# A four-layer graph network on one core: overflow records loaded in one piece, and the side work of a layer-1 block spread over the slots of the block before it

## The chip, the core and the metric

The kernel runs on one core of one Trainium2 chip. The metric is the device time of one execution in microseconds (us), the median of several executions. The core has five engines with an instruction queue each: TensorE (PE in the profile; PEld is its weight load), VectorE (DVE), ScalarE (ACT), GpSimd (POOL) and SyncE (SP), which here only issues transfers. An engine takes its queue in order: an instruction that waits holds up all that stands behind it.

## The reference, cut to what matters

A node table x of 3125 nodes with 256 numbers passes through four layers. Each layer adds a graph step, a mixing step and then a feed-forward step. The change touches the graph step of layer 1 and the preparation of its lists.

```
x   = x + L0_gnn(xn, src, dst) + L0_mix(xn);    x = x + L0_ffn(layernorm(x))
xn  = layernorm(x)
x   = x + L1_gnn(xn, edge_index, edge_type_7, weights) + L1_mix(xn)
x   = x + L1_ffn(layernorm(x))
...  # layers 2 and 3 likewise, with edge weights
```

The layer-1 graph step has 100000 edges of 7 types. Each node adds up, over its incoming edges, the source's row times the matrix of the edge's type, and divides what arrives by each type by the number of such edges (at least 1). Layers 2 and 3 need, for every node, the sums of two edge weights and a count over its incoming edges.

## The kernel before

The nodes are cut into NB = 25 blocks of BS = 125. Edges are held by block in slots of P = 128 edges. For layers 0, 2 and 3 a block has SL = 37 slots (25 regular, OV = 12 overflow); for layer 1 the edges are ordered anew, and a block has L1S = 34 slots (25 regular and 9 overflow).

**Overflow records.** Edges that do not fit layer 1's regular slots are written as records of four numbers to a table `lov_d` in device memory. They wait there in `lrec_d`, with their places in `lpos_d`. `scatter_overflow` (L2334, called 25 times from L2224 to L2225 in `fast_layer0`, ahead of `mix0`) loads 12 columns of places (`lpos`, L2337) and of records (`lrec`, L2339) through SP and then issues 12 indirect writes on POOL (L2341), 300 in all. The tiles have two buffers each. `mix0` follows in the same pool, and its PE, DVE and ACT work can run beside the writes. `lists1` reads `lov_d` back at the start of layer 1.

**Layer 1.** `fast_layer1` first multiplies all nodes by the seven matrices into a table `y_d` of N*7 rows. Then comes the loop of L2451 to L2466. For each of the 34 slots of a block it gathers 128 rows of `y_d` with an indirect transfer from POOL (`rows`, L2461, seen under the helper's line L665), makes a weighted one-hot matrix on DVE (`hot`, L2463), and multiplies the two on PE into the block's sum `agg` (L2465, two matmul records for a slot). After the 34 slots DVE adds `agg` to x (L2466). `rows` has 20 buffers and `hot` 8: the gather of a slot needs the matmul of 20 slots earlier to be done.

**Side work.** The weights of a block's slots, `l_w`, come from `weights1` (L2379 to L2421): seven groups of up to five slots, for each a one-hot `l_hot` on DVE (L2389, two buffers) and five matmuls (L2392) that count the types of each node; then one inversion of the counts (L2395 to L2404); then seven look-ups, each with a broadcast load `hotl` on SP (L1971), a comparison on DVE (L2411) and up to five matmuls (L2414); two multiplications and reductions to `l_w` (L2417, L2419). `node_sums` (L2238 to L2258) makes the sums that layers 2 and 3 need: eight groups with a one-hot `dsthot` on DVE (L2233) and up to five matmuls each (L2250, 37 in all), then a transpose and two small operations.

The loop is written so that the whole side work of block j stands before the slots of block j-1:

```
for j in range(NB + 1):
    if j < NB:
        ws[j] = weights1(k, gp, o, j)
        node_sums(k, gp, j)
    ...
    i = j - 1
    for s in range(L1S): ...   # gather, hot, matmul
```

A scheduler places the instructions of each engine, with the written order as priority and the readiness of their inputs as it models it; the pools decide which buffer an instruction must wait for. In the program as built, each engine's order differs from the written one. On PE, the counting matmuls L2392 of the coming block stand as one bunch of 34 at the end of a block's slots, and the look-ups and node sums stand in bunches of 5 to 20 among the slots of the next. DVE's order follows the same pattern. POOL's queue in the loop holds only gathers, and SP's only the `hotl` loads.

After the loop come the rest of `mix1` (a few of its first operations already lie within the last two blocks) and `ffn1`.

Of the kernel before, what the change touches and what calls it, by code (L numbers as in the profile page):

```python
# [7 lines left out]
F32 = mybir.dt.float32  # L8
BF16 = mybir.dt.bfloat16
I32 = mybir.dt.int32  # L10
AF = mybir.ActivationFunctionType
ALU = mybir.AluOpType
AX = mybir.AxisListType
# [4 lines left out]
D = 256  # L18
E = 100000
BS = 125  # L20
NB = N // BS
P = 128
# [458 lines left out]
def psum(k):  # L481
    return k.mm.tile([P, 512], F32, name="mm")
# [78 lines left out]
def bc(ap, shape):  # L561
    return ap.to_broadcast(shape)
# [1500 lines left out]
def fast_layer0(k):  # L2063
# [157 lines left out]
            if start is not None:  # L2221
                gathers(start)
    with tc.tile_pool(name="l0m", bufs=1) as mp:
        for i in range(NB):  # L2224
            scatter_overflow(k, mp, i)  # L2225
        mix0(k, mp, None, xt)
    ffn0(k)

# [9 lines left out]
def node_sums(k, pool, i):  # L2238

    nc, e = k.nc, k.e  # L2240
    ab = pool.tile([P, SL, 7], BF16, name="ns_ab", bufs=2)
    split3(k, pool, e.ew[:, i, :], ab[:, :, 0:3], [P, SL], "ns_a")
    split3(k, pool, e.ew1[:, i, :], ab[:, :, 3:6], [P, SL], "ns_b")
    nc.vector.memset(ab[:, :, 6:7], 1.0)
    ps = psum(k)
    for s0 in range(0, SL, LQ):
        n = min(LQ, SL - s0)
        hd = dst_hot(k, pool, i, s0, n)
        for u in range(n):
            nc.tensor.matmul(ps[:7, :BS], ab[:, s0 + u, :], hd[:, u, :BS], start=s0 + u == 0,  # L2250
                             stop=s0 + u == SL - 1)
    t = pool.tile([7, BS], F32, name="ns_t", bufs=2)
    nc.scalar.copy(t, ps[:7, :BS])
    pt = k.tp.tile([P, 4, P], F32, name="tp")
    nc.tensor.transpose(pt[:BS, 0, :7], t, k.ident[:7, :7])
    nc.vector.tensor_reduce(e.nd[:BS, i, 0:2], pt[:BS, 0, :6].rearrange("p (a t) -> p a t", t=3),
                            AX.X, ALU.add)
    nc.vector.tensor_copy(e.nd[:BS, i, 2:3], pt[:BS, 0, 6:7])  # L2258


def hot_src(k, pool, e, i, s0, n):
# [69 lines left out]
        nc.sync.dma_start(e.lrec_d, lrec)  # L2331


def scatter_overflow(k, pool, i):  # L2334
    nc, tc, e = k.nc, k.tc, k.e
    lpos = pool.tile([P, OV], I32, name="lpos", bufs=2)
    nc.sync.dma_start(lpos, e.lpos_d[:, i * OV:(i + 1) * OV])  # L2337
    lrec = pool.tile([P, OV, 4], F32, name="lrec", bufs=2)
    nc.sync.dma_start(lrec, e.lrec_d[:, i * OV:(i + 1) * OV, :])  # L2339
    for c in range(OV):  # L2340
        st = nc.gpsimd.indirect_dma_start(  # L2341
            out=e.lov_d, out_offset=bass.IndirectOffsetOnAxis(ap=lpos[:, c:c + 1], axis=0),
            in_=lrec[:, c, :], in_offset=None)
        tc.declare_no_dep(st.ins, group="scatter_l", reason="each edge has a place of its own")
        tc.add_to_no_dep_group("scatter_l", st.ins)
# [30 lines left out]
LG = 5  # L2376


def weights1(k, pool, o, j):  # L2379

    nc = k.nc
    oh = pool.tile([P, L1S, 7], BF16, name="ty_hot", bufs=2)
    nc.vector.tensor_tensor(oh, bc(o.ty[:, j, :, None], [P, L1S, 7]),
                            bc(k.iotab[:, None, :7], [P, L1S, 7]), op=ALU.is_equal)
    cnt = k.agg.tile([P, 512], F32, name="agg")[:7, :BS]
    for s0 in range(0, L1S, LG):
        n = min(LG, L1S - s0)
        S = pool.tile([P, LG, P], BF16, name="l_hot", bufs=2)
        nc.vector.tensor_tensor(S[:, :n, :], bc(o.slb[:, j, s0:s0 + n, None], [P, n, P]),  # L2389
                                bc(k.iotab[:, None, :], [P, n, P]), op=ALU.is_equal)  # L2390
        for u in range(n):
            nc.tensor.matmul(cnt, oh[:, s0 + u, :], S[:, u, :BS], start=s0 + u == 0,  # L2392
                             stop=s0 + u == L1S - 1)
    ct = pool.tile([7, BS], F32, name="l_ct", bufs=2)
    nc.scalar.copy(ct, cnt)  # L2395
    pt = k.tp.tile([P, 4, P], F32, name="tp")
    nc.tensor.transpose(pt[:BS, 0, :7], ct, k.ident[:7, :7])
    inv = pool.tile([BS, 7], F32, name="l_inv", bufs=2)
    nc.vector.tensor_scalar(inv, pt[:BS, 0, :7], 1.0, None, op0=ALU.max)
    nc.vector.reciprocal(inv, inv)  # L2400
    inv3 = pool.tile([BS, 7, 3], BF16, name="l_inv3", bufs=2)
    split3(k, pool, inv, inv3, [BS, 7], "l_i")
    w = pool.tile([P, L1S], F32, name="l_w", bufs=2)
    for h0 in range(0, L1S, 4 * LG):  # L2404
        m = min(4 * LG, L1S - h0)
        pw = psum(k)
        for s0 in range(h0, h0 + m, LG):
            n = min(LG, h0 + m - s0)
            ST = pool.tile([P, LG * P], BF16, name="hotl", bufs=3)
            bcast_rows(k, ST[:, :n * P], o.slT_d, j, s0, n)  # L2410
            nc.vector.tensor_scalar(ST[:, :n * P], ST[:, :n * P], k.part, None, op0=ALU.is_equal)  # L2411
            for u in range(n):
                c = s0 + u - h0
                nc.tensor.matmul(pw[:, c * 21:(c + 1) * 21], ST[:BS, u * P:(u + 1) * P],  # L2414
                                 inv3.rearrange("p a t -> p (a t)"), start=True, stop=True)
        t = pool.tile([P, 4 * LG, 7, 3], F32, name="l_t", bufs=2)
        nc.vector.tensor_tensor(t[:, :m], pw[:, :m * 21].rearrange("p (s a t) -> p s a t", a=7, t=3),  # L2417
                                bc(oh[:, h0:h0 + m, :, None], [P, m, 7, 3]), op=ALU.mult)
        nc.vector.tensor_reduce(w[:, h0:h0 + m], t[:, :m].rearrange("p s a t -> p s (a t)"), AX.X,  # L2419
                                ALU.add)  # L2420
    return w  # L2421


def fast_layer1(k):
    nc, tc, I = k.nc, k.tc, k.ins
    T = 7
    with tc.tile_pool(name="l1g", bufs=1) as gp:
        o = lists1(k, gp)
        xn, xt = k.fresh_norm(gp)
        y_d = k.dpool.tile([N * T, D], F32, name="y_d")  # L2430
        yv = y_d.rearrange("(n t) d -> n (t d)", t=T)
        with tc.tile_pool(name="l1y", bufs=1) as yp:
            wt = yp.tile([P, T, 2, D], F32, name="wt")
            nc.sync.dma_start(wt.rearrange("p t c o -> p (t c) o"),
                              I["L1_gnn_weights"].rearrange("(a p) o -> p a o", p=P))
            for b in range(NB):
                y = yp.tile([BS, T, D], F32, name="y", bufs=2)
                for t in range(0, T, 2):
                    n = min(2, T - t)
                    ps = psum(k)  # L2440
                    pv = ps[:BS, :n * D].rearrange("p (t d) -> p t d", d=D)
                    for c in range(2):
                        nc.tensor.matmul(pv, xt[:, c, b * BS:(b + 1) * BS], wt[:, t:t + n, c, :],
                                         start=c == 0, stop=c == 1)
                    evac(k, y[:, t:t + n, :], pv)
                rows_out(k, yv, b, y.rearrange("p t d -> p (t d)"))
        with tc.tile_pool(name="l1m", bufs=1) as mp:
            k.e.dlb = gp.tile([P, NB, SL], BF16, name="dlb")
            nc.vector.tensor_copy(k.e.dlb, k.e.dl)
            ws = {}  # L2450
            for j in range(NB + 1):  # L2451
                if j < NB:
                    ws[j] = weights1(k, gp, o, j)
                    node_sums(k, gp, j)
                if j == 0:
                    continue
                i = j - 1
                agg = k.agg.tile([P, 512], F32, name="agg")[:BS, :D]
                for s in range(L1S):
                    G = gp.tile([P, D], F32, name="rows", bufs=20)  # L2460
                    gather(k, G, y_d, o.yidx[:, i, s:s + 1])  # L2461
                    S = gp.tile([P, P], F32, name="hot", bufs=8)
                    nc.vector.tensor_scalar(S, k.iota, o.sl[:, i, s:s + 1], ws[i][:, s:s + 1],  # L2463
                                            op0=ALU.is_equal, op1=ALU.mult)
                    nc.tensor.matmul(agg, S[:, :BS], G, start=s == 0, stop=s == L1S - 1)  # L2465
                nc.vector.tensor_tensor(k.x[:, i, :], k.x[:, i, :], agg, op=ALU.add)  # L2466
            mix1(k, mp, xn, xt)
    ffn1(k)

# [84 lines left out]
def split3(k, pool, src, out, shape, name):  # L2554

    nc = k.nc
    r = pool.tile(shape, F32, name=name + "_r", bufs=2)
    nc.vector.tensor_copy(out[..., 0], src)
    nc.vector.tensor_tensor(r, src, out[..., 0], op=ALU.subtract)
    nc.vector.tensor_copy(out[..., 1], r)  # L2560
    nc.vector.tensor_tensor(out[..., 2], r, out[..., 1], op=ALU.subtract)  # L2561
# [260 lines left out]
```

## Time and profile before

| | us |
|---|---|
| Runs: median (lowest to highest of 3) | 9158.93 (9139.79 to 9187.19) |
| Profiled execution: its own time | 9142.26 |
| Span within it | 9140.2 |
| Overflow writes, first to last | 1995.1 to 2389 |
| Layer-1 loop, first gather to last matmul | 3110 to 4503 |

The profile gives for each engine its busy time and share of the span; a strip of 40 slices, each 228.5 us here, with the busy share in tenths; groups of instructions by line, with count, busy time, mean duration in ns and the idle time ahead of them with its releaser; a list of waits in a chosen stretch (engine, tile and line, what ended the wait, total, times, longest); a table of windows with the busy time of each engine, PE's granted clock, the DMA share and GB/s; and a timeline, with the start, the time, the engine and line, and in square brackets the idle time before an instruction and what ended it. "issue" is idle time in which the profile shows nothing waited for; "remote" is a release that it can't name. The layer-1 loop lies in slices 14 to 20 of 40.

### The profile page before, as it was taken

Reading aid. Unit: us, or ns where it says so; the run is one execution under the profiler, and the core shown is the slowest. Engines: PE = TensorE matmul, PEld = TensorE weight load, DVE = VectorE, ACT = ScalarE, POOL = GpSimd, SP = SyncE. Lnnn points to the kernel's source line nnn. Section 1 sums busy time; section 2 is a strip of 40 time slices with the busy share of each in tenths; the row PEclk is TensorE's granted clock in tenths of the full one; section 3 lists DMA queues with packets and bytes.
Section 4 is the critical chain, followed back from the end, with each engine's and each line's share of the span. In section 5 each row is a group of like instructions: output and inputs, shape, how many; then the busy total and the mean of one; then the engine's idle time right before and its main releaser. Section 6 shows DMA issues by size and latency. Waiting matters only on the chain. (4 is left out here: it accounts for less than half of the span.)

```text
span 9140.2 us, 90939 instructions
## 1 busy us (share of the span) xinstructions
PE 6246.5 (68%) x30915; PEld 4571.4 (50%) x30915; DVE 4900.0 (54%) x12476; ACT 1717.6 (19%) x4057; POOL 2252.8 (25%) x2188
## 2 busy tenths in 40 slices
PE   0736888871488755555577887649936666668899
PEld 0724666650244433333456666338825555555455
DVE  9966777751233344444654343741157777775311
ACT  0013444530111000000024444212200000002232
POOL 0001222237300266666402432020032222210000
PEclk9967999985677866766689998759967877779899
DMA  0013333320000333333202222035532222220000
GB/s 18 10 40 98 83 86 82 83 51 4 2 13 30 124 104 99 99 98 101 69 11 66 56 54 52 0 92 173 167 83 67 67 67 66 65 51 20 11 11 22
DMA packets 399982, 570.48 MB, mean 62 GB/s; under 512 B 129911, under 2 KB 322875, under 8 KB 395161
## 3 DMA queue, kind: packets, MB, share of 16 engines
q0 software_dynamic: 107456, 246.32, 12.0%
q1 hardware_dynamic: 292054, 318.25, 12.0%
q8 instruction: 249, 4.08, 0.2%
q14 instruction: 223, 1.83, 0.1%
HBM read 485.78 MB, written 78.47 MB: 62 GB/s over the span
## 5 line engine op out<-in xcount | busy, mean ns | idle before, releaser
L665 POOL DMA_INDIRECT rows<-y_d,l_yidx x850 | 861.1, 1013 | 1246.1 <-DMA kln_weight<-in_L_mix_kln_weight_dram 721.3
L2465 PE MATMUL agg<-rows,hot 128*125 128x256 f32 x1700 | 555.3, 470 | 107.0 <-DVE hot L2463 68.6
L665 POOL DMA_INDIRECT xt<-xp_d,e_idx x300 | 310.6, 1035 | 1135.6 <-PE agg L2704 999.4
L665 POOL DMA_INDIRECT rows<-h_d,e_idx x300 | 306.1, 1020 | 679.5 <-PE agg L2505 393.1
L2465 PEld LDWEIGHTS agg<-rows,hot 128*125 128x125 f32 x1700 | 354.6, 226 | 217.7 <-DVE hot L2463 86.6
L2139 PE MATMUL mm<-er,hotd 125*128 125x258 bf16 x1875 | 319.9, 278 | 193.5 <-DVE jk L2111 133.3
L2483 ACT ACTIVATE whot<-dsthot,e_ew 128x128 f32<-128x128 bf16 x925 | 333.1, 397 | 397.3 <-PE mm L2498 175.4
L2182 ACT ACTIVATE whot<-dsthot,prob 128x128 f32<-128x128 bf16 x925 | 358.8, 401 | 216.8 <-DVE jk L2111 75.7
L2233 DVE TENSOR_TENSOR dsthot<-dlb,iotab 128x640 bf16<-128x640 bf16 (+1 forms) x400 | 306.8, 771 | 130.1 <-remote 108.2
L2463 DVE TENSOR_SCALAR hot<-iota,l_sl,l_w 128x128 f32<-128x128 f32 x850 | 261.1, 363 | 196.8 <-PE agg L2465 130.3
L2502 PE MATMUL agg<-A,dense 125*125 125x256 f32 x1250 | 340.5, 428 | 30.0 <-DVE dense L76 15.4
L2183 PE MATMUL agg<-z,whot 128*125 128x257 f32 x1250 | 356.0, 426 | 6.1 <-ACT whot L2182 6.1
L2686 PE MATMUL mm<-A,hots 125*128 125x256 f32 x1250 | 352.0, 429 | 0.0
L2695 PE MATMUL agg<-msg,whot 128*125 128x260 f32 x1250 | 325.8, 399 | 30.8 <-DVE msg L2689 30.8
L2341 POOL DMA_INDIRECT lov_d<-lrec,lpos x300 | 302.8, 1009 | 152.0 <-issue 91.2
L665 POOL DMA_INDIRECT xn<-el_d,e_idx x156 | 165.1, 1058 | 678.0 <-PE agg L2183 345.9
L2139 PEld LDWEIGHTS <-hotd 125*128 125x128 bf16 x1875 | 181.4, 98 | 274.7 <-issue 224.1
L2617 PE MATMUL mm<-m,hotd 125*128 125x12 bf16 x925 | 28.8, 173 | 409.3 <-DVE m L2561 409.3
L1686 DVE SCALAR_TENSOR_TENSOR x<-mm,gate_lg,x 125x256 f32<-125x256 f32 x200 | 94.6, 484 | 398.8 <-PE mm L545 398.8
L2392 PE MATMUL agg<-l_hot,ty_hot 128*7 128x125 bf16 x850 | 102.9, 282 | 298.5 <-DVE l_hot L2389 223.8
L2111 DVE SCALAR_TENSOR_TENSOR jk<-mm,attn 128x258 bf16<-128x258 f32 x625 | 264.4, 423 | 79.1 <-ACT z L2144 37.6
L2502 PEld LDWEIGHTS agg<-A,dense 125*125 125x125 f32 x1250 | 258.6, 215 | 86.2 <-DVE dense L76 20.2
(683 smaller groups left out, 14262.4 us busy)
## 6 DMA issues: line engine op xcount, KB each, us to landing
w<-in_L_ffn_W_dram SPq DMA_DIRECT2D x64, 1024.0 KB
hotd<-dlT_d SPq DMA_DIRECT2D x25, 1184.0 KB
hotd<-dlT_d SPq DMA_DIRECT2D x175, 160.0 KB
hotl<-lslT_d SPq DMA_DIRECT2D x150, 160.0 KB
y_d<-y SPq DMA_DIRECT2D x25, 875.0 KB
hots<-slT_d SPq DMA_DIRECT2D x125, 160.0 KB
hots_r<-slT_d SPq DMA_DIRECT2D x150, 128.0 KB
rows<-y_d,l_yidx POOLq DMA_INDIRECT x850
```

The costliest lines, as they stand in the source:

```text
L665: k.nc.gpsimd.indirect_dma_start(out=out, out_offset=None, in_=table, in_offset=bass.IndirectOffsetOnAxis(ap=idx, axis=0))
L2111: nc.vector.scalar_tensor_tensor(jk, z, 0.0, at, op0=ALU.max, op1=ALU.mult, accum_out=b.score[:, s:s + 1])
L2139: nc.tensor.matmul(z, DT[:BS, u * P:(u + 1) * P], b.er3[:, j, :], start=j == 0, stop=False)
L2182: nc.scalar.activation(pd, hd[:, u, :], AF.Copy, scale=b.p[:, s:s + 1])
L2183: nc.tensor.matmul(b.agg, pd[:, :BS], rows[:, u, :D + 1], start=s == 0, stop=s == SL - 1)
L2233: k.nc.vector.tensor_tensor(t[:, :n, :], bc(k.e.dlb[:, i, s0:s0 + n, None], [P, n, P]), bc(k.iotab[:, None, :], [P, n, P]), op=ALU.is_equal)
L2341: st = nc.gpsimd.indirect_dma_start(out=e.lov_d, out_offset=bass.IndirectOffsetOnAxis(ap=lpos[:, c:c + 1], axis=0), in_=lrec[:, c, :], in_ ...
L2465: nc.tensor.matmul(agg, S[:, :BS], G, start=s == 0, stop=s == L1S - 1)
L2483: nc.scalar.activation(pd, hd[:, u, :], AF.Copy, scale=e.ew[:, i, s0 + u:s0 + u + 1])
L2502: nc.tensor.matmul(agg, A[:BS, u, :BS], hv[:, s0 + u, :], start=s0 + u == 0, stop=False)
L2686: nc.tensor.matmul(pg[:, (u - u0) * D:(u - u0 + 1) * D], STs[s0 // GQ][:BS, u * P:(u + 1) * P], av[:, s0 + u, :], start=True, stop=True)
L2695: nc.tensor.matmul(agg, pd[:, :BS], M[:, u, :], start=s0 + u == 0, stop=False)
```

## The change

1. `scatter_overflow` loads all 300 columns of `lpos` (128 x 300) and `lrec` (128 x 1200) with one transfer each, and then issues the same 300 indirect writes. The tiles have one buffer each.
2. `weights1` and `node_sums` no longer run their work but return it as steps: 7 count, 1 invert, 7 look, 1 begin, 8 add, 1 end, 25 in all. The loop places the steps of block j+1 between the slots of block j, 0 or 1 after each slot. Block 0's steps run ahead of the loop.
3. `rows` has 16 buffers instead of 20, `hot` 10 instead of 8, `l_hot` 3 instead of 2.

```diff
-        for i in range(NB):
-            scatter_overflow(k, mp, i)
+        scatter_overflow(k, mp)
...
-    lpos = pool.tile([P, OV], I32, name="lpos", bufs=2)
-    nc.sync.dma_start(lpos, e.lpos_d[:, i * OV:(i + 1) * OV])
-    lrec = pool.tile([P, OV, 4], F32, name="lrec", bufs=2)
-    nc.sync.dma_start(lrec, e.lrec_d[:, i * OV:(i + 1) * OV, :])
-    for c in range(OV):
+    C = NB * OV
+    lpos = pool.tile([P, C], I32, name="lpos")
+    nc.sync.dma_start(lpos, e.lpos_d)
+    lrec = pool.tile([P, C, 4], F32, name="lrec")
+    nc.sync.dma_start(lrec, e.lrec_d)
+    for c in range(C):
...
-        S = pool.tile([P, LG, P], BF16, name="l_hot", bufs=2)
+        S = pool.tile([P, LG, P], BF16, name="l_hot", bufs=3)
...
+    groups = list(range(0, L1S, LG))
+    return ([lambda s0=s0: count(s0) for s0 in groups] + [invert]
+            + [lambda s0=s0: look(s0) for s0 in groups])
...
+    return [begin] + [lambda s0=s0: add(s0) for s0 in range(0, SL, LQ)] + [end]
...
-            for j in range(NB + 1):
-                if j < NB:
-                    ws[j] = weights1(k, gp, o, j)
-                    node_sums(k, gp, j)
-                if j == 0:
-                    continue
-                i = j - 1
+            def side(j):
+                if j >= NB:
+                    return []
+                ws[j] = gp.tile([P, L1S], F32, name="l_w", bufs=2)
+                return weights1(k, gp, o, j, ws[j]) + node_sums(k, gp, j)
+            for f in side(0):
+                f()
+            for j in range(NB):
+                steps = side(j + 1)
                 agg = k.agg.tile([P, 512], F32, name="agg")[:BS, :D]
                 for s in range(L1S):
-                    G = gp.tile([P, D], F32, name="rows", bufs=20)
+                    G = gp.tile([P, D], F32, name="rows", bufs=16)
...
-                    S = gp.tile([P, P], F32, name="hot", bufs=8)
+                    S = gp.tile([P, P], F32, name="hot", bufs=10)
...
                     nc.tensor.matmul(agg, S[:, :BS], G, start=s == 0, stop=s == L1S - 1)
+                    n = len(steps) * (s + 1) // L1S - len(steps) * s // L1S
+                    for f in steps[len(steps) * s // L1S:len(steps) * s // L1S + n]:
+                        f()
```

In the program as built after the change, the largest bunch of side matmuls between two slots on PE holds 20 instead of 35, and most hold 5; the longest run of side operations between two `hot` on DVE is 6 instead of 24. POOL's order of writes and gathers is the one of before. SP has 48 transfers fewer. The block's addition to x stands on DVE ahead of the counting steps of the block after next.

## The prediction

> **What bounds the kernel now.** I read the page first: the totals, then the strip.
>
> ```profile
> span 9140.2 us, 90939 instructions
> PE 6246.5 (68%) x30915; PEld 4571.4 (50%) x30915; DVE 4900.0 (54%) x12476; ACT 1717.6 (19%) x4057; POOL 2252.8 (25%) x2188
> PE   0736888871488755555577887649936666668899
> POOL 0001222237300266666402432020032222210000
> ```
>
> No engine bounds the whole; each stage has its own limit. The change touches two stages: slices 8 to 10 (overflow writes) and 14 to 20 (layer-1 loop). In the loop POOL is at 6 tenths and PE at 5: neither is full. The groups give POOL's and PE's part of it.
>
> ```profile
> L665 POOL DMA_INDIRECT rows<-y_d,l_yidx x850 | 861.1, 1013 | 1246.1 <-DMA kln_weight<-in_L_mix_kln_weight_dram 721.3
> L2465 PE MATMUL agg<-rows,hot 128*125 128x256 f32 x1700 | 555.3, 470 | 107.0 <-DVE hot L2463 68.6
> ```
>
> 850 gathers of 1013 ns are 861 us of a loop of 1393 us (3110 to 4503). The 721.3 is the wait ahead of the first gather and is no part of the loop. The list of waits for that stretch says what POOL waits for (us in total, times, longest), and what PE waits for:
>
> ```profile
> POOL rows L665 <- PE agg L2465: 213.5, 128, 10.5
> POOL rows L665 <- issue: 168.4, 543, 1.9
> POOL rows L665 <- remote: 102.7, 95, 3.0
> ...
> PE agg L2392 <- DVE l_hot L2389: 221.7, 62, 17.6
> PE mm L2250 <- DVE dsthot L2233: 136.6, 27, 7.4
> PE agg L2392 <- issue: 72.7, 13, 12.0
> PE agg L2465 <- DVE hot L2463: 68.6, 51, 2.9
> ```
>
> "issue" is 0.3 us ahead of an ordinary gather. The longest waits are for the slot matmul L2465: no row buffer is free. And PE, which should free it, waits most in the side work. The timeline of POOL shows one such place, then the ordinary pace:
>
> ```profile
> 3304.85 0.98 POOL L665 DMA_INDIRECT rows<-y_d,l_yidx  x1 [9.48 <-PE agg L2465]
> 3306.13 0.95 POOL L665 DMA_INDIRECT rows<-y_d,l_yidx  x1 [0.30 <-issue]
> 3307.39 0.95 POOL L665 DMA_INDIRECT rows<-y_d,l_yidx  x1 [0.30 <-issue]
> ```
>
> PE and DVE ahead of it, from the same timeline:
>
> ```profile
> 3293.99 0.42 DVE L2466 TENSOR_TENSOR x<-x,agg 125x256 f32<-125x256 f32 x1 [7.82 <-remote]
> ...
> 3297.03 0.69 PE L2392 MATMUL agg<-l_hot,ty_hot 128*7 128x125 bf16 x5 [11.67 <-issue]
> ...
> 3303.36 1.22 PE L2465 MATMUL agg<-rows,hot 128*125 128x256 f32 x2 [1.32 <-DVE hot L2463]
> ```
>
> The slot matmul before that last line ended at 3284.2: 19 us with none. For 11.7 us PE stood in its bunch for an `l_hot` that was queued on DVE behind the addition to x, itself held 7.8 us by a release the profile can't name; 6.3 us more went to the rest of the bunch.
>
> So a gather can go every 1.25 us (0.95 + 0.30). By the starts of all 850, 21 of the 25 blocks have one wait of over 3 us, nearly always after the block's 20th gather: 20 buffers are full, and the block's first matmul is queued behind the 34 counting matmuls of the next block, which wait for `l_hot`. These 21 waits are 174 us beyond the 0.30 each. Another 45 waits of 1 to 3 us, mostly after the 31st gather, are 83 us. Longer gathers (1013 against 950 ns) are 54 us, the rest small. Typical block: 56.5 us, of which 42.5 (34 x 1.25) is POOL's floor.
>
> The windows say whether another engine would be next:
>
> ```profile
> 3600.00:4000.00 400.00, 211.62 (x1230) 148.59 (x1229) 191.59 (x555) 3.57 (x14) 241.96 (x239) 0.70 0.35 99
> ```
>
> Columns: length, busy PE, PEld, DVE, ACT, POOL, PE clock, DMA share, GB/s. Over the whole loop PE is busy 769 us (31 a block), DVE 671 (27 a block): both under 42.5.
>
> [...] the last gather starts at 4495.3 and its matmul is over at 4503.2, with seven slots of matmuls caught up in the last 5 us. I take up to 8 us from gather to matmul. [...] gathers last 0.95 us at the median, some 1.4 to 1.7. The DVE operations stay the same in number, so I keep those 54 us. [...] The trace has 0.70 in the loop, and a slot's matmul pair takes 0.70 or 1.22 us.
>
> **Part by part.**
>
> *Steps between slots.* Nothing is removed: 34 + 34 + 37 side matmuls and 7 + 7 + 8 wide one-hots a block stay, and so do the seven `hotl` loads on SP, whose queue in the loop holds nothing else. What changes is order. PE's longest bunch between two slot matmuls shrinks from 35 to 20, most to 5; DVE's longest side run between two `hot` from 24 operations to 6. Five matmuls behind one `l_hot` are 0.82 + 5 x 0.28 = 2.2 us; twenty are 20 x 0.18 to 0.28 = 4 to 6 us, and six DVE operations 3 to 4 us. With 16 buffers POOL runs 16 x 1.25 = 20 us ahead of PE; 8 of them cover the landing, 12 remain. Each of these bunches fits in 12, so the 6.3 us of bunch come off those 19, and the 11.7 us at the addition to x, which I leave as it is, plus 2.2 for the first five matmuls exceed the cover by about 2 us a block. The 174 us go, but some of that comes back: of the 83 us in the 45 shorter waits I take away only half, 41, and the 42 left are those 2 us a block. (DVE's waits at the addition to x are 24, 120 us, "remote", up to 12.2 each; all that follows on DVE is queued behind it, the next block's `hot` and `l_hot` above all, then PE, then POOL.) Sum: 174 + 41 = **215 us** off the loop, 1393 to 1178. A second way gives nearly the same. Block 25, beside which no next block's side work lies, took 46.6 us; 25 x 46.6 + 8 for the last landing = 1173. The floor is 25 x 42.5 + 54 + 8 = 1125, a gain of 268.
>
> *Buffers.* 16 `rows` for 20 take 4 x 1.25 = 5 us of cover. If a stall of more than 12 us is left in every block, each is 5 us longer than with 20: up to 25 x 5 = 125 us back. `hot` 10 lets DVE run 12.5 us ahead of POOL's pace instead of 10; `l_hot` 3 gives one group more. I take 0 for all three, with 0 to +125.
>
> *Block 0's steps* stay ahead of its slots, as before: 0. *mix1 and ffn1* start when the loop ends; their length doesn't change: 0.
>
> *Records in one piece.* 48 of SP's 50 transfers of 6 or 24 KB go. POOL never waits for them after the first: 300 writes go steadily at 1.28 us (0.97 + 0.30) from 1995.1 to 2389, and the only wait is before the first. That first write now waits for 154 + 614 KB; at the 99 GB/s of the window shown this is about 8 us, where the small pair took 3.7 (issued from 1991.4): 4 us later. And `mix0`'s weights are queued behind it on SP. The writes then end near 2393. `mix0` beside them goes on to about 2550, so 0 with that cover, +4 without it. On the other side: during the writes `mix0` crawls, with waits of up to 51 us on DVE and ACT whose releaser the profile can't name ("remote"), and its passes take 9.6 us each once the writes are over, against some 55. If the 25 small load pairs caused that, `mix0` would end with the writes: 2550 - 2393 = 157 us less. Nothing ties the two: loads come every 15.3 us, the waits last about 46. I take 0, with -157 to +4.
>
> Sum: -215 on the profiled execution's 9142.3 gives 8927. The median of the runs lies 17 us above that execution; I take half, and predict **8935**.
>
> **Rivals.**
>
> *(a) The coupling of DVE and PE becomes the pace: slower.* From 4457 to 4470 PE and DVE have little side work, and still a slot takes 2.1 to 3.6 us: DVE makes one `hot`, waits for PE, PE makes one slot and waits.
>
> ```profile
> 4459.91 0.35 DVE L2463 TENSOR_SCALAR hot<-iota,l_sl,l_w 128x128 f32<-128x128 f32 x1 [1.78 <-PE agg L2465]
> 4462.03 0.53 DVE L2463 TENSOR_SCALAR hot<-iota,l_sl,l_w 128x128 f32<-128x128 f32 x1 [1.77 <-PE agg L2465]
> 4464.87 0.35 DVE L2463 TENSOR_SCALAR hot<-iota,l_sl,l_w 128x128 f32<-128x128 f32 x1 [2.31 <-PE agg L2465]
> ```
>
> With side work after most slots, such a round trip could come at every step. Today a slot costs 1393 / 850 = 1.64 us in the mean; the rival decides from there. If half the slots took 2.4 and half 1.37 (46.6 / 34), the loop is 850 x 1.89 = 1607: +214, so 9142 + 214 = 9356. Against it: 10 `hot` buffers, and in most of the trace PE takes slots in runs of several.
>
> *(b) No change: landing sets the pace.* If rows land no faster than 1.6 us a slot, emptier queues gain nothing: 9142 to 9159. For it: waits called "remote" that may be late transfers. Against: the waits of `agg` for `rows` are 10.5 us in the whole loop, and the DMA share is 0.35. Nor would it be a change of the text that a scheduler undoes: the built order differs as said.
>
> *(c) mix0 is freed as well:* 8927 - 157 = 8770.
>
> **How the numbers follow.** A difference within 0.5%, about 46 us, is what a measurement of this kernel can tell from no change. Main case 0.77: gains of 80 to 268, so 8875 to 9080. (c) 0.08. (b) 0.07. (a) 0.08. Faster 0.77 + 0.08 = 0.85, same 0.07, slower 0.08. The range reaches down to 8820, for a main case in which longer gathers vanish too (-54), and up to 9100; outside are (c), (a) and most of (b)'s upper part, some 0.2.
>
> **What would show it.** Right: POOL's waits for `agg` in the loop fall from 213 us to under 60 with none over 5; blocks of 46 to 48 us; the loop about 1180 us long with POOL at 7 tenths or more; writes still at 1.28 us from a start some 4 us later, `mix0` as long as before. Wrong: one wait of 5 us or more left in every block (then which bunch precedes it), or `hot` waiting for `agg` by far more than the 130 us of now (rival a), or PE waiting for `rows` (rival b).

## The result, and the profile after

The changed kernel takes 9027.74 us in the median (9012.22 to 9036.69, 4 runs), against 9167.19 us of the kernel before (9139.79 to 9187.19, 4 runs): a ratio of 0.9848, 95% interval 0.9818 to 0.9878. That is 139 us less, where 215 to 224 were forecast. The profiled execution has a span of 9034.8 us, 105.4 less than the 9140.2 of before, which was near the lowest of its runs.

The totals and the strip of the changed kernel:

```profile
span 9034.8 us, 91075 instructions
PE 6300.0 (70%) x30915; PEld 4549.1 (50%) x30915; DVE 4879.1 (54%) x12476; ACT 1720.2 (19%) x4057; POOL 2262.3 (25%) x2188
PE   0736888882388866666588887549837666678899
POOL 0001222227500066666303332020032222210000
```

Busy time is the one of before on every engine, within 1%. POOL is still at 6 tenths in the loop, where the prediction wanted 7. The costliest groups of the loop (busy, mean ns, idle time ahead):

```profile
L665 POOL DMA_INDIRECT rows<-y_d,l_yidx x850 | 864.9, 1018 | 1120.5 <-DMA hotl<-lslT_d 726.5
L2489 PE MATMUL agg<-rows,hot 128*125 128x256 f32 x1700 | 615.6, 486 | 49.9 <-issue 35.2
```

The waits within the loop, now 3137 to 4403 (engine, line, what ended the wait, us, times, longest), first POOL's, then PE's, then DVE's:

```profile
POOL rows L665 <- issue: 167.8, 533, 1.9
POOL rows L665 <- remote: 85.6, 63, 3.3
POOL rows L665 <- PE agg L2489: 72.8, 129, 2.9
```

```profile
PE mm L2253 <- DVE dsthot L2232: 93.6, 18, 17.8
PE mm L2427 <- DVE hotl L2423: 91.3, 20, 9.6
PE mm L2427 <- issue: 60.8, 30, 7.4
```

```profile
DVE hotl L2423 <- DMA hotl<-lslT_d: 159.0, 49, 13.2
DVE l_t L2432 <- remote: 147.4, 18, 21.0
```

POOL's waits for `agg` fell from 213.5 to 72.8 us, and the longest from 10.5 to 2.9. PE's waits for `l_hot` (221.7) are gone from the top of the list, and so are DVE's 120 us at the addition to x. In their place PE waits at the look-ups and node sums, and DVE at the look-ups' loads and at `l_t`. By the starts of the gathers, POOL's idle time beyond 0.30 us a gather:

| | before | after |
|---|---|---|
| first to last gather | 1385.0 | 1257.9 |
| waits over 3 us | 174.0 (21) | 3.1 (1) |
| waits of 1 to 3 us | 82.9 (45) | 120.2 (71) |
| smaller ones | 13.3 | 15.9 |
| gathers themselves | 861.0 | 865.0 |

The two kinds of wait are different things. A gather may start when the slot matmul that reads the old rows of its buffer is done, 20 slots back before the change and 16 after it. In the kernel before, all 21 waits over 3 us end 0.27 us after the recorded end of that matmul: the matmul came late, and GpSimd was released at once. Of the 45 waits of 1 to 3 us, 44 begin only after that matmul has ended, and the gather starts 7.1 us after its end in the median. One of them (before):

```profile
3169.32 4.26 PE L2465 MATMUL agg<-rows,hot 128*125 128x256 f32 x19
3180.95 0.95 POOL L665 DMA_INDIRECT rows<-y_d,l_yidx  x1 [2.65 <-PE agg L2465]
```

The matmul pair that this gather needs is among the 19 records of the upper line and ended at 3171.4, 9.5 us before the gather starts. After the change 63 of the 71 waits of 1 to 3 us are of this kind; the median over all 71 is 6.8 us. So the change took away the waits for late matmuls, and left those that end late though the matmul, by the record, is long over.

The loop gained 127 us. It also begins 27 us later, of which 21 come before the first record load, in a part of layer 0 that the change doesn't touch; the rest of the kernel is 5 us shorter.

### The profile page after: what moved, and what is told of

It reads as the page before. It is cut to its first block, busy times and chain, and to the rows that moved or that the text cites. A ratio compares the mean times of both kernels' runs of the same rounds, so it can differ in the third digit from the quotient of the medians.

```text
span 9034.8 us, 91075 instructions
## 1 busy us (share of the span) xinstructions
PE 6300.0 (70%) x30915; PEld 4549.1 (50%) x30915; DVE 4879.1 (54%) x12476; ACT 1720.2 (19%) x4057; POOL 2262.3 (25%) x2188
## 5 line engine op out<-in xcount | busy, mean ns | idle before, releaser
L2489 PE MATMUL agg<-rows,hot 128*125 128x256 f32 x1700 | 615.6, 486 | 49.9 <-issue 35.2
L2144 ACT COPY z<-mm 128x256 f32<-128x256 f32 x625 | 227.8, 373 | 388.3 <-PE mm L2142 274.0
L2713 PEld LDWEIGHTS mm<-A,hots 125*128 125x128 f32 x1250 | 274.6, 222 | 48.2
```

Source lines behind the costliest of these rows:

```text
L2713: nc.tensor.matmul(pg[:, (u - u0) * D:(u - u0 + 1) * D], STs[s0 // GQ][:BS, u * P:(u + 1) * P], av[:, s0 + u, :], start=True, stop=True)
```

## The experiments

The runs fell on two kinds of chip: the kernel before takes 9120 to 9167 us where the change was first measured and in all groups below but the last, and 8398 to 8411 us in the last. Each is compared with the kernel before on its own chip. No chip appears in both groups, and each was used at one time only, so "kind of chip" may also be a condition that it was in. As it turned out, this difference carries the explanation.

### The two halves of the change

**Steps only:** the loads in 25 pieces again, the steps and buffers of the change.

```diff
-        scatter_overflow(k, mp)
+        for i in range(NB):
+            scatter_overflow(k, mp, i)
```

> The layer-1 steps and buffers of the change, with the overflow records still loaded in 25 pieces. The profile of the changed kernel has the first overflow write 22 us later than before (2017.5 against 1995.1), but the first load for it is issued 21 us later too, after a layer 0 that took longer. Theory 1 (the one-piece load costs nothing and that shift is a difference between executions): 9015 to 9040, as the changed kernel, and from the first load to the first gather of layer 1 the 1119 to 1125 us that both profiles show. Theory 2 (the one-piece load or what it does to layer 0 costs 20 us): 9000 to 9015.

Measured: 9024.94 us, ratio 0.9882 (0.9852 to 0.9913) to the 9132.18 of before on this chip; loop 1258.0. From the first load to the first gather: 1115 us.

**Records only:** the kernel before with the reverse edit.

> The kernel before with the overflow records loaded in one piece and nothing else changed. Theory 1: no difference, 9150 to 9180, loop of 1393 us, mixing step of layer 0 as slow as before. Theory 2: 15 to 25 us slower, 9180 to 9190. Rival (c) of the prediction (the small load pairs make the mixing step crawl): 9010 to 9030.

Measured: 9139.71 us, ratio 1.0001 (0.9984 to 1.0019); loop 1392.7. The one-piece load is worth nothing, neither a cost nor a gain: none of the 157 us by which rival (c) shortens the mixing step shows, and rival (c) falls. The 21 us in layer 0 are a difference between executions (the first load starts at 1985 and 1993 in these two). The whole gain is that of the loop.

### Buffers in the loop

```diff
-                    G = gp.tile([P, D], F32, name="rows", bufs=16)
+                    G = gp.tile([P, D], F32, name="rows", bufs=20)
```

> The changed kernel with 20 row buffers again instead of 16. GpSimd's idle time beyond 0.30 us a gather was 139 us in the loop of the changed kernel, in some 72 waits of 1 to 3 us, against 270 before. Theory A (the look-ups stand on VectorE for broadcast loads that have only three buffers; the waits have a length of their own): the 20 buffers give 5 us more cover and nearly all waits of 1 to 3 us vanish too: loop 1258 to about 1170, 8935 to 8960. Theory B (four buffers don't matter, since the stalls are of 10 us and more and come in rows): loop 1220 to 1258, 8990 to 9027.

Measured: 9038.43 us, ratio 0.9881 (0.9843 to 0.9918); loop 1263.4, idle beyond 0.30 still 139. Four more buffers do nothing; theory A falls, and the loop is 5 us above the range of theory B.

```diff
-        ST = pool.tile([P, LG * P], BF16, name="hotl", bufs=3)
+        ST = pool.tile([P, LG * P], BF16, name="hotl", bufs=6)
```

> The changed kernel with six buffers for the broadcast loads of the look-ups (hotl) instead of three, so that six of a block's seven loads can be issued before the first look-up has run. Theory A (late broadcast loads are what holds VectorE, and through it the slots): VectorE's 159 us of waits for these loads fall to under 40, GpSimd's idle time beyond 0.30 us a gather from 139 to 30 to 70 us, loop 1165 to 1200, 8930 to 8970. Theory C (late signals from TensorE, named remote in the profile, are the cause and the loads only stand next to them): the waits move to l_t and l_inv, loop 1230 to 1260, 9000 to 9030.

Measured: 9004.05 us, ratio 0.9867 (0.9828 to 0.9907), which can't be told from the change; loop 1251.1, idle beyond 0.30 at 120. DVE's longest waits in this kernel's loop:

```profile
DVE l_t L2432 <- remote: 215.1, 27, 16.5
DVE e_nd L2261 <- PE tp L2260: 66.2, 12, 10.0
DVE l_t L2432 <- PE agg L2489: 59.6, 12, 11.6
```

The waits for the loads, 159 us, are gone from the top, and `l_t` waits 68 us more under "remote": theory A falls here too, theory C stands. In all four kernels with steps a block takes 50 us.

### Without side work, and without gathers

```diff
+                if j > 0:
+                    def plain():
+                        nc.vector.memset(ws[j], 1.0)
+                        nc.vector.memset(k.e.nd[:BS, j, :], 1.0)
+                    return [plain]
```

> The changed kernel without the side work of blocks 2 to 25: the weights of their slots and their node sums are set to 1 instead (left out: 24 x 25 steps with their loads). All runs so far with the steps have 50 us a block, whatever the buffers (16 or 20 rows, 3 or 6 hotl), and 45 to 48 us for the last block, beside which no side work lies. Theory E (TensorE's queue sets the pace: 32 us busy and some 16 us of waiting at side matmuls in every block): without them TensorE has 34 x 0.72 = 25 us a block, so GpSimd sets the pace at 34 x (0.30 + 0.95 to 1.02) = 42.5 to 45 us, 1070 to 1130 us for the loop, 8860 to 8910 in all. Theory F (gathers land no faster than 1.4 us each): 47 us a block or more, loop above 1170.

Measured: 8914.02 us, loop 1212.5, 48.5 us a block, idle beyond 0.30 at 140. Theory E misses by 3.5 us a block and more: the whole side work costs only 2 us a block now. Theory F's figures fit; it comes back below as theory L. (72 us of the total come from operations of `mix1` that moved into the loop; the rest after the last gather is 4568 us against 4640.) POOL still stands 140 us in waits, with hardly anything beside the slots. All its 83 waits of 1 to 3 us begin after the slot matmul that it needs has ended, and the gather starts 13.8 us after that end in the median (3.4 to 20.9). An example:

```profile
3594.93 2.25 PE L2494 MATMUL agg<-rows,hot 128*125 128x256 f32 x4
3616.68 0.35 DVE L2492 TENSOR_SCALAR hot<-iota,l_sl,l_w 128x128 f32<-128x128 f32 x1 [0.98 <-PE agg L2494]
3616.91 0.95 POOL L665 DMA_INDIRECT rows<-y_d,l_yidx  x1 [1.89 <-PE agg L2494]
```

The first of the two slots in the upper line ended at 3595.99; the gather that takes over its buffer starts 20.9 us later, together with a `hot` that also waited for TensorE.

```diff
-                    G = gp.tile([P, D], F32, name="rows", bufs=16)
-                    gather(k, G, y_d, o.yidx[:, j, s:s + 1])
+                    if s == 0:
+                        G = gp.tile([P, D], F32, name="rows", bufs=16)
+                        gather(k, G, y_d, o.yidx[:, j, s:s + 1])
```

> The changed kernel with one gather a block; all 34 slots use its rows (left out: 33 of 34 gathers). Side work and slots as in the changed kernel. Theory E (the two queues hold each other up by their order alone): the blocks stay near 45 to 50 us. Theory H (signals that TensorE has finished reach the other engines late while GpSimd issues indirect transfers: the profile has ScalarE start 9 us after the count matmuls it needs, all engines but GpSimd idle): without gathers the waits shrink to under 5 us a block and the block falls to TensorE's 32 to 38 us, loop 800 to 950.

Measured: 8460.44 us. The window of the loop (length, busy PE, PEld, DVE, ACT, POOL, PE clock, DMA share, GB/s) and PE's longest waits in it:

```profile
3120.00:3819.00 699.00, 654.15 (x4274) 422.36 (x4272) 627.38 (x1944) 13.30 (x51) 17.26 (x18) 0.97 0.14 42
```

```profile
PE mm L2427 <- DVE hotl L2423: 12.3, 25, 1.5
PE agg L2490 <- DVE hot L2488: 9.7, 38, 0.3
```

28 us a block, PE at 0.97 of its clock, hardly a wait: PE and DVE, with all their work of the change, need 28 us for what takes them 50 beside gathers. Part of that is the clock: in the loop of the changed kernel it is 0.74 (0.70 in the one before), and PE is busy 807 us, 32 a block. Their work and what they wait for from each other don't make 50 us (theory E). Theory H has the right direction, but the loop is shorter than its 800 to 950 us. What is left is that the gathers slow the engines that they feed: by late reports (theory H) or by late rows (F, L).

### Where the waits come from

The traces that were already there decide about late rows. A gather shows as 48 DMA packets. The last of them ends 2.45 us after the gather's start in the median before the change, 2.53 after it and 2.41 without side work, and at most 6.0 us after it; on the other chips of the last group it is 2.48 and 2.55, at most 5.9. Rows come as early where the waits are as where they aren't: theories F and L fall. What remains is that TensorE's completion comes late to the engines that wait for it. Whether it is TensorE that finishes late or only its report, the profile can't tell, since the ends of matmuls in it are modelled; "late report" stands for both below.

A place in the loop of the changed kernel shows what such a wait looks like; PE's side of the timeline, and the instruction of ACT that it waits for:

```profile
3516.65 0.39 PE L2403 MATMUL agg<-l_hot,ty_hot 128*7 128x125 bf16 x4
3516.96 0.70 PE L2489 MATMUL agg<-rows,hot 128*125 128x256 f32 x2
...
3525.95 0.25 ACT L2408 COPY l_ct<-agg 7x125 f32<-7x125 f32 x1 [18.00 <-remote]
3526.25 0.37 PE L2410 MATMUL tp<-ident,l_ct 7*125 7x7 f32 x1 [8.59 <-ACT l_ct L2408]
```

ACT's copy needs the last counting matmul, which by the record ended at 3517.0. It starts 8.9 us later, and in the built program it waits for no other engine and no transfer. From 3517.8, when DVE ends its last operation, only POOL works. PE's queue stands behind L2410: the next slot matmul has had its rows since 3507.8 and its `hot` since 3517.1, and starts at 3526.55, right after L2410. In other blocks the same copy starts 0.09 us after the same matmul. The passes of layer 0's mixing step, where the next copy starts some 46 us after the last matmul, look alike. Two runs took that place, as no slot waits for rows there.

```diff
+        z = mp.tile([1, 1], F32, name="kv_z", bufs=2)
+        nc.vector.tensor_copy(z, kv[0:1, n - 1, 0:1])
+        pt = k.tp.tile([P, 4, P], F32, name="tp")
+        for _ in range(4):
+            nc.tensor.matmul(pt[:1, 0, :1], z, k.ones[0:1, 0:1], start=True, stop=True)
```

> The changed kernel with four 1x1 matmuls (into a spare PSUM tile, needed by nothing) behind the kv matmuls of each pass of layer 0's mixing step, which during the overflow writes stands 46 us in each of its passes after these matmuls. Theory G (a finished matmul is reported only when more work enters TensorE): the kv matmuls are reported at once, the passes take 10 instead of 56 us, and the step ends soon after the writes: 130 to 160 us less, 8870 to 8900. Theory H (the report is late because GpSimd issues indirect transfers, whatever follows on TensorE): no difference, 9000 to 9035.

Measured: 9014.10 us, ratio 0.9883 (0.9848 to 0.9918): no gain. PE in one pass:

```profile
2164.59 1.16 PE L858 MATMUL mm<-kv 125*128 125x128 f32 x8
2165.68 0.28 PE L865 MATMUL tp<-ones,kv_z 1*1 1x1 f32 x6
2167.49 0.16 PE L865 MATMUL tp<-ones,kv_z 1*1 1x1 f32 x1 [1.53 <-issue]
2169.59 0.16 PE L865 MATMUL tp<-ones,kv_z 1*1 1x1 f32 x1 [1.94 <-issue]
2235.47 3.70 PE L545 MATMUL mm<-wkv,xt 128*125 128x512 f32 x4 [65.72 <-issue]
```

More work behind the last matmul doesn't bring the report: theory G falls. It makes a pass longer, which theory H had not foreseen:

```profile
2234.72 0.58 ACT L74 COPY kv<-mm 125x512 f32<-125x512 f32 x1 [70.31 <-remote]
2313.18 0.58 ACT L74 COPY kv<-mm 125x512 f32<-125x512 f32 x1 [68.56 <-remote]
```

A pass takes 78.4 us here and shows 28 matmul records; in the changed kernel it takes 56.0 us with 20, and the first ones 16.8 us with 6. (One pass between them shows 14 records and takes 56.0 too.) That is 2.80 us a record each time, for a 1x1 matmul as for one of 128x512. So the delay beside the writes is not a fixed time: it is a pace at which TensorE's matmuls are done or reported. The total stays as it was because the crawl ends with the writes, and a pass after them takes some 10 us. The loop keeps no such single pace: 68 slot records a block take 48.5 us alone and 50 us with 105 side records between them.

```diff
-    for c in range(C):
+    for c in range(0, C, 2):
         st = nc.gpsimd.indirect_dma_start(
```

> The changed kernel with every second overflow write left out (150 instead of 300, so some edges of layer 1 are missing). Theory H: the crawl of the mixing step lasts as long as the writes, 196 us less, and the passes after it take 10 us each: the step ends 150 to 165 us earlier, 8870 to 8890 in all. If the crawl has nothing to do with the writes: no difference, 9000 to 9035.

Measured: 8845.17 us, 276 less than the kernel before on its chip (9120.94), and 169 less than the kernel of the run above, which differs from the changed one by the idle matmuls alone and ran on the same chip. The last write starts at 2183.2. ACT's evacuations in the mixing step:

```profile
2118.95 0.58 ACT L74 COPY kv<-mm 125x512 f32<-125x512 f32 x1 [50.28 <-issue]
2174.95 0.58 ACT L74 COPY kv<-mm 125x512 f32<-125x512 f32 x1 [50.18 <-remote]
2198.86 0.58 ACT L74 COPY kv<-mm 125x512 f32<-125x512 f32 x1 [18.09 <-remote]
2210.96 0.58 ACT L74 COPY kv<-mm 125x512 f32<-125x512 f32 x1 [6.27 <-PE mm L858]
```

50 us in each pass while writes go. The last late copy starts 15.7 us after the last write and 211 us after the first; in the changed kernel that takes 416 (2017.5 to 2433.8). The crawl is as long as the writes, as theory H has it; the total moved a little more than its 150 to 165 us.

### On the other chips

> The changed kernel with 8 row buffers instead of 16. Theory L (a row is usable only some 20 us after its gather starts, so 16 or 20 buffers just cover it): 8 buffers allow 8 gathers in 20 us, 2.5 us a slot, loop about 2100 us. Theory H (the waits end when GpSimd pauses for a buffer): with 8 buffers it pauses sooner and oftener but for less; loop 1200 to 1400 us. Theory of the prediction (16 buffers are 20 us of cover, of which landing takes 8; with 8 buffers 2 us remain): every wait of TensorE reaches GpSimd, loop 1400 to 1700.

```diff
-                    G = gp.tile([P, D], F32, name="rows", bufs=16)
+                    G = gp.tile([P, D], F32, name="rows", bufs=8)
```

Measured: 8402.94 us on a chip where the kernel before takes 8411.18 (8400.19 to 8441.91). The loop's POOL waits and the passes of the mixing step beside the writes (1949 to 2308):

```profile
POOL rows L665 <- issue: 113.6, 373, 0.3
POOL rows L665 <- PE agg L2489: 81.3, 267, 0.3
POOL rows L665 <- PE mm L2253: 19.5, 64, 0.3
```

```profile
1960.65 0.59 ACT L74 COPY kv<-mm 125x512 f32<-125x512 f32 x1 [2.06 <-PE mm L858]
1968.76 0.58 ACT L74 COPY kv<-mm 125x512 f32<-125x512 f32 x1 [2.06 <-PE mm L858]
```

None of these waits of POOL is over the ordinary 0.3 us; a block takes 45.0 us, the loop 1125.7, and a pass of the mixing step 8.1 us with the writes going on. All three expectations are wrong for this chip, because what they explain isn't there.

**Buffers only:** the kernel before with 16 `rows`, 10 `hot` and 3 `l_hot`, its side work in one piece.

> The kernel before with 16 row, 10 hot and 3 l_hot buffers, the side work still in one piece. Prediction: each of the some 21 waits of 9 us becomes 5 us longer, loop 1385 to about 1500. Theory H (GpSimd's waits end some us after it pauses, so 4 buffers fewer only let it pause earlier; but a bunch of 19 us without a slot is real work and waiting): loop 1420 to 1500.

Measured: 8415.05 us, ratio 1.0005 (0.9991 to 1.0018) to the kernel before; loop 1120.9. POOL's and DVE's waits in the loop:

```profile
POOL rows L665 <- issue: 121.9, 400, 0.3
POOL rows L665 <- PE agg L2465: 75.7, 248, 0.4
```

```profile
DVE x L2466 <- PE agg L2465: 193.8, 24, 10.2
```

The bunch of 34 counting matmuls is there, DVE still waits up to 10.2 us at the addition to x, and with four row buffers fewer POOL doesn't feel it (its longest wait in the loop is one of 1.9 us). Both expectations, 1420 to 1500 us, miss by 300 us and more. So on this chip the bunch, which the prediction takes for the cause, costs nothing.

**Unread gathers:** 33 of the 34 gathers of a block go into buffers that nothing reads.

```diff
+                    if s == 0:
+                        G = gp.tile([P, D], F32, name="first", bufs=2)
+                        gather(k, G, y_d, o.yidx[:, j, s:s + 1])
+                    else:
+                        U = gp.tile([P, D], F32, name="rows", bufs=14)
+                        gather(k, U, y_d, o.yidx[:, j, s:s + 1])
```

> The changed kernel with every block's slots multiplied by the rows of the block's first gather; the other 33 gathers are still issued, into 14 buffers that nothing reads (left out: the use of their rows). With one gather a block TensorE and VectorE took 28 us a block with hardly a wait; with all gathers, read, 50 us. Theory L (the rows themselves come late, so slots wait for them): gathers that nobody reads don't matter, GpSimd issues them at 1.25 to 1.32 us without a wait, TensorE's work of a block takes 28 to 32 us again, and the loop ends with the last gather, 42.5 to 45 us a block, 1065 to 1125 us. Theory H (what TensorE has finished is reported late while GpSimd issues indirect transfers, until GpSimd pauses): now GpSimd never pauses, and TensorE, VectorE and ScalarE stand in waits of 10 to 50 us as they do beside the overflow writes: the slots take longer than the gathers, and the loop is longer than 1258 us.

> The kernel of e11_unread once more (33 of a block's 34 gathers unread, the slots multiplied by the rows of the first; left out: the use of their rows). The three runs sent with e11_unread were on a chip on which the kernel before takes 8411 us, and on which neither the crawl beside the overflow writes nor the waits of GpSimd in the loop are there (45 us a block with 8 row buffers). Where the kernel before takes 9110 to 9190: theory L (rows come late): gathers go at 1.25 to 1.32 us, TensorE takes 28 to 32 us a block, and the loop ends with the gathers, 1065 to 1125 us. Theory H (late reports while GpSimd issues): the slots stand in waits of 10 to 50 us and the loop is longer than 1258 us. Where the kernel before takes 8411 again: loop about 1100 us, and L and H stay apart only by the overflow writes.

Measured: 8583.95 and 8572.11 us, on two chips of the other kind (the second has 8397.56 before), the unread gathers from 2857 to 3956 in the second. There PE stands 523 us in 18 waits for a block's first gather, which is queued on POOL behind the 33 unread ones of the block before. What the runs were for, telling late rows from late reports where the waits exist, they couldn't do; the DMA packets above do it.

## Why the prediction was right, and where it was wrong

- **The total** lies in the range, with the right sign; the gain is 62% of the forecast.
- **The long waits go: right, and for the reason given.** 174 us in 21 waits became 3.1 in one, against the 174 of the sum: 171. Each of the 21 ended 0.27 us after the matmul that it needed, so a matmul that stood late in PE's queue made them, as the prediction had it. That the order alone makes them is not so: on the other chips the order of before, with 16 buffers, has none.
- **The waits of 1 to 3 us: the term that was mis-sized.** The sum took 41 us off the 83. They grew by 37, to 120 us in 71 waits. These 78 us are nearly the whole miss of 88 in the loop (215 against 127); 4 are longer gathers, 3 the small waits, the other 3 the long waits.
- **The step behind that term.** The prediction took these waits as a rest of the side work's bunches, and halved them without a reason of their own. But 44 of the 45 began after the matmul that they waited for had ended: it was not a matmul standing late in PE's queue that held them. The 120 us at the addition to x (19 waits, not 24) did vanish, but waits of the same kind appeared at the look-ups, `l_t` and the node sums. Taking away one place (six `hotl` buffers), adding cover (20 `rows`), or leaving out the whole side work (48.5 us a block) left POOL 120 to 140 us of waits. With the gathers gone they were gone.
- **The cover.** "8 of them cover the landing" is a misreading: the last gather of the loop before, started at 4495.3, had landed 2.5 us later, and the rest of the 8 us to the end of its matmul is not landing.
- **The floor: right elsewhere.** The 42.5 us a block plus longer gathers, 1125 us in all, is what the other chips reach (1121 and 1126), with or without steps. On the chips of the forecast no kernel with all its gathers got below 48 us a block in the mean; of the 55.4 us a block before, the change left 50.3, close to the 48.5 without side work.
- **Block 25 as a second way** agreed only by chance: its 46.6 us have side work absent, but 25 blocks without side work took 48.5 each.
- **The records: right.** 0 was taken, 1.0001 measured. The load in one piece let the first write start 5.8 us after its issue, against 4.1.
- **The buffers.** "0 to +125" for fewer `rows`: 20 for 16 changed nothing where the waits are (loop 1263.4 against 1257.9), and 16 for 20 nothing where they aren't (ratio 1.0005).
- **Rivals.** (a): `hot` waits for `agg` 21.5 us instead of 130, so DVE and PE are not coupled through `hot`. (b): PE's waits for rows stayed small (6.3 us), and the rows land in 2.5 us. (c): fell with the records run, but its suspicion was near a truth: the crawl belongs to the writes, not to their loads.
- **The longer gathers.** The prediction kept their 54 us because DVE's operations stay the same in number; that DVE's operations lengthen gathers was its assumption. Between 3200 and 4300 a gather takes 1019 ns in the changed kernel (755.0 us for 741) and 961 without the side work (741.7 us for 772), with DVE busy 572 us in the first and 340 in the second. So, as an estimate, some 49 us of the loop (850 x 58 ns) go with the side work; whether with DVE's operations or with the `hotl` loads, which are gone too, isn't shown. The delays behind TensorE are another matter.

**What is shown and what is not.** Shown: on one kind of chip, engines that wait for TensorE start late, up to 9 us (ACT's copy) and 21 us (POOL) in the loop and some 46 us in the passes beside the overflow writes; rows are not late there; the delay goes away with the indirect transfers on the same kind of chip, and is absent with them on the other. The change gained its 127 us there by taking away the one long stop that most blocks had, in which GpSimd waited for a slot matmul queued late on PE; the waits behind late reports stayed. Open: whether TensorE finishes late or only reports late; by what path an indirect transfer delays it, and why at 2.80 us a matmul record beside the writes; and what makes the chips differ. Whether the changed kernel itself is faster than before on the other chips wasn't measured; with 8 `rows` it is within the spread of before there.

## What to carry to other kernels

A wait for a full buffer points at a slow consumer. Before spreading the consumer's work, look when the instruction that frees the buffer ended: here the waits that ended 0.27 us after it were of order, and the new order took them from 174 us to 3.1; those that ended 7 us after it in the median were not, and stayed. And take the producer away once: here that shows at once that the consumer needs 28 us and not 50. More buffers (20 for 16: a loop of 1263.4 against 1257.9) bought nothing here, where the waits come back in every block. Repeat a gain on another chip before building on it: waits that the profile calls "remote" may belong to the chip, or to the state it is in, and not to the code.

## What the runs showed of the hardware that I had not expected

- With GpSimd issuing indirect writes of 128 records every 1.31 us, the engines behind TensorE go on at 2.80 us a matmul record, whatever its size (16.8 us for 6 records, 56.0 for 20, 78.4 for 28), until 15 to 29 us after the last write. On the other chips, with writes every 1.34 us, a pass takes 8.1 us, and ACT's copy has 2.06 us of idle time ahead of it, against 50 us in the passes beside the writes of the changed kernel.
- An indirect gather of 131 KB has landed 2.4 to 2.6 us after its start in the median on both kinds of chip.
- Halving 300 indirect writes shortened the kernel by about 170 us: on these chips nearly all of the 197 us that 150 writes take is on the path that sets the end.
- The same kernel takes 9120 to 9167 us on some chips and 8398 to 8411 on others, 8% less. Between the profiles of before and of the buffers-only kernel the difference is 726 us; 264 of it lie in the loop (1385 against 1121) and 167 between the first overflow write and the first gather of layer 1 (1115 against 948).
